# Row transpositions at the seam of image attention and output stage: which engine empties a block, in which order, and from which PSUM pool

## Chip, cores and metric

One core of a Trainium2 chip. The metric is the device time of one execution in microseconds, given as the median of several runs; the profile is one further execution on the same chip type, recorded by the hardware profiler.

## What is computed

The reference passes an image batch `x` of 4 x 56 x 56 x 128 through four layers, each added to its input after a group norm: `x = x + layer(gn(x))`. Layer 0 is a window attention with an MLP, layer 1 an edge and node layer, layer 2 a Fourier operator block with an attention over images, layer 3 a convolution along one axis with sums over rows and columns. The change lies in layer 2, between these lines and what follows them:

```python
attn_w = jax.nn.softmax(scores, axis=-1)
out = jnp.einsum('bhts,bhsd->bhtd', attn_w, vs)       # image attention, in the spectral domain here
...
projd = _fno_layer(out, wP, wPs, bPs, (H, W))
attention = _inorm(projd + xa, norm_g[1], norm_b[1])  # output stage: back transform, norms, two more
an = _inorm(attention, norm_g[2], norm_b[2])          # spectral layers, Gelu, then layer 3
```

H and W are 56, the four samples have 56 images each, and everything is float32.

## The kernel before, in words

The program is a sequence of stages. `build` (L2687) runs layers 0 and 1 sample by sample, then the spectra, the scores and the softmax of layer 2, then `attend` (L1802), then `outputs` (L2630), which does the rest of layer 2 and layer 3.

`attend` goes through 24 turns (four groups of eight columns, three products, two pairs of samples). In a turn ACT copies a piece of the spectrum into a two-bank PSUM tile (`u_px`, two buffers, L1844), DVE (L1869, reading that tile) and GpSimd (L1871) multiply it by broadcast factors, and PE sums the products with the attention weights in a one-bank tile (`u_po`, two buffers, L1874). A third kind of tile (`x_po`, two banks, one buffer) serves the mixing of images beside it. The results go to `st.y`, which is 128 partitions by (pair of samples, 32 columns, real and imaginary part, 56). The last sums of a turn of the third kind are two DVE additions that read `u_po` (L1884, or L1901 after the last turn). The PSUM pool `u_ps` (8 banks) is opened and closed inside `attend`.

`outputs` opens its own PSUM pool `o_ps`: one-bank tiles `b` (two buffers) and two-bank tiles `d` (three buffers). It describes its work as some 790 steps, each with an engine, steps that it must follow, and tiles that it takes and gives back; the list `OUTPUT_ORDER` fixes the order in which the steps are issued, and so the order on each engine. PE, ACT, DVE and GpSimd each work through their queue in that order and wait by semaphores where they need another engine's result.

The first steps belong to `attended_rows` (L2569). For each pair of samples it transposes `st.y` in four blocks of eight columns: one PE step of eight transpositions into a `d` tile (L2586), then four copies out of it (L2593), one for each half sample, into that half's tile `o_y` of 112 x 28 x 32. The copies of one block alternate: ACT, DVE, ACT, DVE. Steps 0, 5, 10 and 15 are the transpositions of the first pair, 20, 25, 30 and 35 those of the second; the four numbers after each are its copies.

`half_sample` (L2067) then works on each of eight half samples: a load of the mixed images into `o_a` (L2260, on SP's queue, 0.8 MB as rows of 56 values), a copy of one row of constants into `o_y` on ACT (`put_dc`, L2265), a transform over h on PE (L2114), its copy to SBUF on ACT (L2272), a transform over c on PE (L2131), a DVE sum with `o_a` (L2281), a transform over w on PE (L2145), the spectral products (L2167), the norms (L2198, L2225), and so on. `put_dc` is entered as following all sixteen copies of its pair of samples. Between the first and the second pair's transpositions the first three half samples advance; near the second pair's, ACT also has a root (L2302) and two Gelus with their table loads (L2336), whose result the next transform over w (L2145) reads. The large loads of `x` (L2347) are issued on SP after the second pair's transpositions.

## Time and profile before

| | |
|---|---|
| median of 3 runs | 3626.33 us |
| the runs | 3609.95, 3626.33, 3628.69 us |
| the profiled execution's own time | 3623.46 us |
| its span | 3621.7 us |
| busy in the span: PE, DVE, ACT, GpSimd | 3401.0, 2706.0, 2091.6, 1247.4 us |
| from 3254 us to the end (output stage): PE, DVE, ACT, GpSimd | 337.14, 227.82, 145.45, 222.53 us of 368 us |
| granted PE clock, before and after 3254 us | 0.98, 0.91 |

Times in the profile are microseconds from the span's start. A line of a timeline gives the start, the length, the engine, the source line, the operation, the tile written and those read, the shapes and how many instructions were merged; in brackets stands the idle time of the engine before it and what released it. A float32 matmul appears as two records (two passes), a transposition as one. Tile names lose their buffer numbers.

### The profile page before, as it was taken

To read this page: it belongs to the slowest core of one execution; us is meant where nothing else is said; L and a number is where in the kernel's file an instruction comes from. 1 tells how busy PE (TensorE), PEld (TensorE's weight loads), DVE (VectorE), ACT (ScalarE), POOL (GpSimd) and SP (SyncE) were. 2 spreads that over 40 slices of the span, in tenths; PEclk is the share of its full clock that TensorE was granted. 3 is DMA by queue.
4 is the path that set the end of the run, shared out by engine and by line. 5 is a ranking of instruction groups with operands and counts; after the bars stand their busy time and mean duration, and the time that the engine had idled before them with its cause. 6 is when DMAs were issued, how large, how long until landed. Compare 5 with 4: busy or idle time off the path is not lost.

```text
span 3621.7 us, 80884 instructions
## 1 busy us (share of the span) xinstructions
PE 3401.0 (94%) x36096; PEld 1567.0 (43%) x36096; DVE 2706.0 (75%) x2532; ACT 2091.6 (58%) x2103; POOL 1247.4 (34%) x751
## 2 busy tenths in 40 slices
PE   6999998999999898999989899999898989999998
PEld 4433344553333455333346543334466433336664
DVE  6588859758887786788859658885965768885756
ACT  4688865458887555788856468886542012215432
POOL 1000018500000660000038200001854768874766
PEclk9999999999999999999999999999998999999989
DMA  2243320024442002344400034332021047742201
GB/s 102 48 92 87 91 41 20 20 57 92 93 92 62 20 3 54 76 95 96 93 19 3 20 87 93 87 88 53 26 66 33 1 108 187 181 107 79 63 10 54
DMA packets 98496, 244.51 MB, mean 68 GB/s; under 512 B 64540, under 2 KB 69916, under 8 KB 93244
## 3 DMA queue, kind: packets, MB, share of 16 engines
q0 software_dynamic: 16128, 102.77, 14.0%
q1 hardware_dynamic: 75152, 123.61, 11.6%
q10 hardware_dynamic: 6860, 12.88, 1.3%
q8 instruction: 285, 4.67, 0.5%
q14 instruction: 71, 0.58, 0.0%
HBM read 79.46 MB, written 31.33 MB: 31 GB/s over the span
## 4 chain that ended last, share of the span: by engine, by line
PE 78%; DVE 10%; ACT 4%; issue 4%; POOL 3%; DMA 0%; DVEq 0%; POOLq 0%; SPq 0%; ACTq 0%
PE f_pm L818 17%; PE f_pm L684 15%; PE u_po L1874 8%; PE e_acc L1238 7%; PE q_acc L1732 3%; DVE e_td L1231 3%; PE f_pm L791 2%; PE e_po L1206 2%; PE f_pm L770 2%; ACT f_ring L821 1%; PE o_d L2548 1%; PE f_pm L464 1%; PE o_d L2145 1%; DVE f_acc L673 1%; PE f_pm L715 1%
## 5 line engine op out<-in xcount | busy, mean ns | idle before, releaser
L821 ACT ACTIVATE f_ring<-f_pm 128x1792 f32<-128x1792 f32 (+1 forms) x764 | 1093.9, 1482 | 228.6 <-PE f_pm L818 181.1
L673 DVE TENSOR_TENSOR f_acc<-f_acc,f_ring 128x1792 f32<-128x1792 f32 x468 | 947.7, 2025 | 191.1 <-ACT f_ring L821 160.9
L818 PE MATMUL f_pm<-f_qT,f_kT 32*128 32x448 f32 x5376 | 725.1, 571 | 15.5 <-ACT f_ring L821 5.1
L684 PE MATMUL f_pm<-f_ring,f_va 128*32 128x448 f32 (+1 forms) x6304 | 589.4, 490 | 0.0
L663 POOL DMA_DIRECT2D f_far<-f_ring x112 | 96.6, 862 | 1329.4 <-ACT f_ring L821 1087.9
L1231 DVE TENSOR_TENSOR e_td<-e_pa,e_c 128x1792 f32<-128x1792 f32 x252 | 491.1, 2018 | 14.1 <-ACT e_a L1196 14.1
L1233 POOL TENSOR_TENSOR e_tp<-e_a,e_c 128x1792 f32<-128x1792 f32 x140 | 451.5, 3263 | 101.5 <-PE e_acc L1238 60.0
L818 PEld LDWEIGHTS f_pm<-f_qT,f_kT 32*128 32x128 f32 x5376 | 260.0, 183 | 417.5 <-ACT f_ring L821 305.0
L1238 PE MATMUL e_acc<-e_td,t_shared 32*32 32x448 f32 x8064 | 325.9, 544 | 24.9 <-DVE e_td L1231 24.1
L684 PEld LDWEIGHTS f_pm<-f_ring,f_va 128*32 128x32 f32 x6304 | 163.8, 109 | 410.1 <-issue 397.8
L1869 DVE TENSOR_TENSOR u_ud<-u_px,u_d 112x1792 f32<-112x1792 f32 (+1 forms) x145 | 264.9, 1859 | 43.3 <-PE u_po L1874 35.9
L1235 ACT ACTIVATE e_tp<-e_tp 128x1792 f32<-128x1792 f32 x140 | 233.4, 1694 | 74.0 <-POOL e_tp L1233 74.0
L1871 POOL TENSOR_TENSOR u_up<-xh,u_d 112x1792 f32<-112x1792 f32 (+1 forms) x71 | 238.8, 3390 | 50.4 <-PE u_po L1874 36.3
L1238 PE MATMUL e_acc<-e_tp,t_shared 32*32 32x448 f32 x4480 | 222.8, 544 | 3.1 <-ACT e_tp L1235 2.4
L1874 PE MATMUL u_po<-u_ud,AT 112*64 112x448 f32 x1060 | 218.1, 549 | 6.4 <-issue 6.4
L1238 PEld LDWEIGHTS e_acc<-e_td,t_shared 32*32 32x32 f32 x8064 | 142.2, 103 | 138.5 <-DVE e_td L1231 79.5
L1874 PEld LDWEIGHTS u_po<-u_ud,AT 112*64 112x64 f32 x1060 | 75.6, 139 | 136.8 <-issue 122.5
L1717 POOL TENSOR_TENSOR q_u<-iS,q_g 128x1792 f32<-128x1792 f32 x32 | 102.8, 3236 | 64.9 <-PE s_px L1565 41.8
L1250 ACT COPY e_sums<-e_acc 128x1792 f32<-128x1792 f32 x28 | 46.3, 1652 | 136.4 <-PE e_acc L1238 136.4
L1238 PEld LDWEIGHTS e_acc<-e_tp,t_shared 32*32 32x32 f32 x4480 | 96.7, 103 | 52.9 <-issue 16.4
L728 DVE RECIPROCAL f_den<-f_den 128x448 f32<-128x448 f32 x28 | 82.6, 2951 | 44.1 <-ACT f_den L725 44.1
L1874 PE MATMUL u_po<-u_up,AT 112*64 112x448 f32 x476 | 105.1, 554 | 9.0 <-POOL u_up L1871 9.0
(525 smaller groups left out, 4557.0 us busy)
## 6 DMA issues: line engine op xcount, KB each, us to landing
f_far<-f_ring POOLq DMA_DIRECT2D x112, 896.0 KB, 6.3
u_d<-dd SPq DMA_DIRECT2D x44, 784.0 KB
f_far<-f_ring SPq DMA_DIRECT2D x28, 896.0 KB
xw<-in_x SPq DMA_DIRECT2D x4, 1568.0 KB
x2d<-x SPq DMA_DIRECT2D x4, 1568.0 KB
xat<-x SPq DMA_DIRECT2D x4, 1568.0 KB
x_xs<-xat ACTq DMA_DIRECT2D x32, 196.0 KB
xm<-x_ev ACTq DMA_DIRECT2D x64, 98.0 KB
```

The lines of the kernel that those rows point to most:

```text
L673: nc.vector.tensor_add(e.acc, e.acc, slots(j, c))
L684: nc.tensor.matmul(e.po[heads[h], part], va[o, c, heads[h]], p, start=(c == 0), stop=(c == 23 and part.stop == NB))
L818: nc.tensor.matmul(ss[:, i, :NB], kT[heads[h], c * P:(c + 1) * P], qT[heads[h], blk(j)], start=True, stop=True)
L821: nc.scalar.activation(ring[:, slot:slot + m, :], ss[:, :m, :NB], AF.Exp, scale=scale)
L1231: nc.vector.tensor_tensor(t, am, cm, ALU.max)
L1233: nc.gpsimd.tensor_sub(t, bc(a.rearrange("p (l n) -> p l n", l=8), 1, 4), cm)
L1235: nc.scalar.activation(tf, tf, AF.Relu)
L1238: nc.tensor.matmul(acc[quarters[q], r, :NB], k.ident[o, o], t[o, q].rearrange("p l n -> p (l n)"), start=(g == 0), stop=(g == len(EDGE_TUR ...
L1732: nc.tensor.matmul(acc[bp][i][halves[hb % 2], hb // 2, :NB], x[o], u[o, 8 * hb:8 * hb + 8, :].rearrange("p h t -> p (h t)"), start=first, ...
L1869: nc.vector.tensor_mul(u, bc(px[:, :, :NB], 2, m), dm)
L1871: nc.gpsimd.tensor_mul(u, bc(x, 2, m), dm)
L1874: nc.tensor.matmul(po[64 * b2:64 * b2 + 64, :NB], st.AT[:, 8 * i + h0 + q, 2 * bp + b2, :], u[:, b2, q, :], start=(left == 16), stop=(left ...
```

## The change

Three things, all in the two places where `st.y` is transposed, and in the PSUM pools.

1. Each block is emptied by one engine. For the first pair of samples, blocks 0 and 2 (columns 0 and 16) go to ACT and blocks 1 and 3 to DVE; for the second pair, blocks 0 and 3 go to ACT and 1 and 2 to DVE. The number of copies on each engine is the same as before (eight and eight for each pair).
2. Order. `put_dc` of a half sample follows that half's four copies alone. In the list of steps, each block's copies stand together, the third block's copies are mixed with the fourth's and with `put_dc`, and the first transform over h (step 42) stands directly after the first half's copies.
3. One PSUM pool `l2_ps`, opened in `build`, serves both stages. `u_px` and two of three `d` tiles share a tag with two buffers, `x_po` and every third `d` tile one with one buffer, `u_po` and `b` one with two.

```diff
-def attend(k, I, w, st, dd, xat, xm, softmax, beside):
+def attend(k, I, w, st, dd, xat, xm, softmax, beside, psum):
...
-        psum = es.enter_context(tc.tile_pool(name="u_ps", bufs=2, space=PSUM))
...
-            return psum.tile([P, 2, 512], F32, name="x_po", bufs=1)
+            return psum.tile([P, 2, 512], F32, tag="x", name="x_po", bufs=1)
...
-            px = psum.tile([112, 2, 512], F32, name="u_px")
+            px = psum.tile([P, 2, 512], F32, tag="px", name="u_px")[:112]
...
-            po = psum.tile([P, 512], F32, tag="acc", name="u_po")
+            po = psum.tile([P, 512], F32, tag="b", name="u_po")
...
-    @op("ACT", 0.2, rows.ops + [load_a])
+    @op("ACT", 0.2, rows.of[me] + [load_a])
     def put_dc():
...
+        dve = c0 in ((16, 8) if bp else (8, 24))
...
-            L.pt = pools.psum.tile([P, 2, 512], F32, tag="d", name="o_d", bufs=3).rearrange("p i (c t) -> p (i c) t", c=4)
+            L.pt = pools.banks().rearrange("p i (c t) -> p (i c) t", c=4)
...
-        for i, (b, half) in enumerate(units):
-            def copy_rows(i=i, b=b, half=half, c0=c0, L=L):
+        for b, half in units:
+            def copy_rows(b=b, half=half, c0=c0, L=L, dve=dve):
...
-                (nc.vector.tensor_copy if i % 2 else nc.scalar.copy)(o, L.pt[:112, :, at:at + T])
-            rows.ops.append(plan.add("DVE" if i % 2 else "ACT", 0.4, copy_rows, [p], (), [d]))
+                (nc.vector.tensor_copy if dve else nc.scalar.copy)(o, L.pt[:112, :, at:at + T])
+            rows.ops.append(plan.add("DVE" if dve else "ACT", 0.4, copy_rows, [p], (), [d]))
+            rows.of.setdefault((b, half), []).append(rows.ops[-1])
...
-0 40 119 227 306 10 3 2 1 4 5 13 12 11 14 15 6 9 7 8 18 19 16 17 41 228 120 42 307 121 43 45 44 122 124 229 47
+0 40 119 227 306 5 10 1 2 3 4 6 7 8 9 15 11 16 41 42 12 17 120 13 18 228 14 19 307 121 43 45 44 122 124 229 47
...
-239 73 149 147 74 76 240 20 150 247 25 24 23 22 21 248 77 35 29 27 30 28 37 36 39 26 38 82 31 32 33 34 78 151 83
+239 73 149 147 74 76 240 20 150 247 25 21 22 23 24 248 77 35 26 27 28 29 30 36 37 38 39 82 31 32 33 34 78
+151 83
...
-def outputs(k, w, st, ys, x2d, xm, out):
+def outputs(k, w, st, ys, x2d, xm, out, psum):
...
-        pools.psum = es.enter_context(tc.tile_pool(name="o_ps", bufs=2, space=PSUM))
-        opened = []
+        opened, taken = [], [0]
+
+        def bank():
+            return psum.tile([P, 512], F32, tag="b", name="o_b")
+
+        def banks():
+            taken[0] += 1
+            tag, bufs = ("x", 1) if taken[0] % 3 == 0 else ("px", 2)
+            return psum.tile([P, 2, 512], F32, tag=tag, name="o_d", bufs=bufs)
+        pools.bank, pools.banks = bank, banks
...
+            psum = es.enter_context(tc.tile_pool(name="l2_ps", bufs=2, space=PSUM))
-            attend(k, I, w2, st, dd, xat, xm, last_softmax, conv_weights(k, w2, l2p))
+            attend(k, I, w2, st, dd, xat, xm, last_softmax, conv_weights(k, w2, l2p), psum)
...
-        outputs(k, w2, st, ys, x2d, xm, out)
+        outputs(k, w2, st, ys, x2d, xm, out, psum)
```

More of the change, by code (lines that the diff above doesn't have):

```diff
@@ L2072, in half_sample @@
     nc = k.nc
-    wk, psum = pools.wk, pools.psum
+    wk, bank, banks = pools.wk, pools.bank, pools.banks
     T, G = HH // 2, HH // 8
@@ L2085, in tile_of @@
         return wk.tile(shape, F32, tag=tag, name="o_" + tag, bufs=plan.buffers.get(tag, 6))
-    def bank():
-        return psum.tile([P, 512], F32, tag="b", name="o_b", bufs=2)
-    def banks():
-        return psum.tile([P, 2, 512], F32, tag="d", name="o_d", bufs=3)
     def slots(x, i):
@@ L2438, in last_layer @@
     nc = k.nc
-    wk, psum = pools.wk, pools.psum
+    wk, bank, banks = pools.wk, pools.bank, pools.banks
     V = Env()
@@ L2445, in buf @@
         return n, (b, count[0])
-    def bank():
-        return psum.tile([P, 512], F32, tag="b", name="o_b", bufs=2)
-    def banks():
-        return psum.tile([P, 2, 512], F32, tag="d", name="o_d", bufs=3)
     def tile_of(shape, tag):
@@ L2574, in attended_rows @@
     rows.y, rows.ops, first = {}, [], []
+    rows.of = {}
     units = [(2 * bp + b2, half) for b2 in range(2) for half in range(2)]
```

## The prediction

> **What bounds the kernel now.** I read the busy shares first, then the chain of waits around the end of the image attention, then the timelines of PE, ACT and DVE there, and last the granted clock in windows.

> ```profile
> PE 3401.0 (94%) x36096; PEld 1567.0 (43%) x36096; DVE 2706.0 (75%) x2532; ACT 2091.6 (58%) x2103; POOL 1247.4 (34%) x751
> ...
> PE 78%; DVE 10%; ACT 4%; issue 4%; POOL 3%; DMA 0%; DVEq 0%; POOLq 0%; SPq 0%; ACTq 0%
> ```

> The kernel is bound by PE, so a gap of PE is worth its length. The change touches two places, both in the output stage that begins at 3254 us: the transpositions for samples 0 and 1, right at the seam, and those for samples 2 and 3, near 3302 us. PE's timeline at the first:

> ```profile
> 3250.92 3.18 PE L1874 MATMUL u_po<-u_ud,AT 112*64 112x448 f32 x16
> 3255.44 2.81 PE L2586 MATMUL o_d<-t_shared,y 128*112 128x128 f32 x24 [1.35 <-DVE y L1901]
> 3259.07 1.06 PE L2586 MATMUL o_d<-t_shared,y 128*112 128x128 f32 x8 [0.83 <-DVE o_y L2593]
> 3263.37 6.28 PE L2114 MATMUL o_d<-t_images,o_y 112*128 112x112 f32 x28 [3.23 <-ACT o_y L2265]
> 3269.57 1.60 PE L2131 MATMUL o_d<-o_v,t_images 32*128 32x392 f32 x16
> ```

> The bracket is the idle time before the row and its releaser. PE stands 1.35 us for DVE's last sums of the attention, 0.83 us for a free bank, 3.23 us for the row copies. Then 28 records of L2114 take 6.28 us, where 14 take 1.81 us elsewhere. The copies, two rows of ACT and two of DVE:

> ```profile
> 3256.66 0.56 ACT L2593 COPY o_y<-o_d 112x224 f32<-112x224 f32 x1 [22.40 <-PE o_d L2586]
> 3257.83 0.91 ACT L2593 COPY o_y<-o_d 112x224 f32<-112x224 f32 x2 [0.62 <-DVE o_y L2593]
> 3257.25 0.55 DVE L2593 COPY o_y<-o_d 112x224 f32<-112x224 f32 x1 [1.95 <-ACT o_y L2593]
> 3258.40 0.91 DVE L2593 COPY o_y<-o_d 112x224 f32<-112x224 f32 x2 [0.60 <-ACT o_y L2593]
> ```

> The two engines never overlap on a block; each waits 0.6 us for the other. The second place:

> ```profile
> 3305.81 1.08 PE L2586 MATMUL o_d<-t_shared,y 128*112 128x128 f32 x8 [0.81 <-ACT o_y L2593]
> 3309.23 5.17 PE L2145 MATMUL o_d<-t_images,o_t 128*128 128x64 f32 x28 [2.34 <-ACT o_y L2593]
> 3314.33 3.00 PE L2131 MATMUL o_d<-o_v,t_images 32*128 32x392 f32 x16
> ```

> Here L2145 takes 5.17 us against 3.34 us in later rows, L2131 3.00 against 1.60. The windows say why (columns: stretch, length, busy time of PE, PEld, DVE, ACT, POOL, then granted clock, DMA share, GB/s):

> ```profile
> 3255.83:3259.24 3.41, 2.58 (x25) 2.37 (x23) 1.39 (x3) 1.46 (x3) 0.00 (x0) 1.00 1.28 246
> 3259.24:3262.66 3.42, 0.90 (x8) 0.65 (x6) 1.83 (x5) 1.83 (x4) 0.00 (x0) 1.00 1.32 214
> 3307.04:3310.45 3.41, 1.22 (x11) 1.22 (x11) 0.62 (x2) 3.06 (x7) 0.13 (x2) 1.00 0.76 243
> 3365.06:3368.48 3.42, 1.96 (x10) 0.84 (x12) 3.42 (x5) 0.30 (x2) 3.42 (x2) 1.00 0.00 0
> 3460.60:3494.80 34.20, 33.88 (x158) 25.28 (x160) 14.52 (x34) 12.41 (x17) 12.27 (x9) 0.50 0.00 0
> ```

> The windows at 3259 and 3307, in which PE was busy 0.90 and 1.22 us, are each followed by 6.83 us at clock 0.50 (3262.66 to 3269.49, 3310.45 to 3317.27). Those with 1.96 or 2.58 us busy are not. The last line is a half-clock stretch that lasts 34 us although PE is hardly idle in it.

> [...] here 2.4 us of transpositions filled the window at 3255.83 and the clock stayed at 1.00, so I count them as busy. [...]

> **The change part by part, first place.** Times are on the clock of the profiled execution.

> One PSUM pool. The first transpositions read columns finished long before; what they wait for is the closing of the attention's pool, whose last reader is DVE L1901. In the built program's waits this one is gone, since their buffers are those of the attention's older tiles. They start behind the last L1874, at 3254.10 instead of 3255.44: 1.35 us. Nothing else in the attention's instruction rows or waits differs, so no cost there. The same three large buffers turn in the same order of taking, so nothing new comes to wait for a bank.

> One engine for each block. A copy costs 0.55 us alone; two in a row 0.91, three 1.28, so 0.37 us for each further one and 1.66 us for four. First copy 1.22 us after its block's first transposition (3256.66 less 3255.44). ACT: block 0 from 3255.32 to 3256.98. DVE: block 1 from about 3256.2 (its transpositions begin 0.86 us later), past L1901, which ends at 3255.3, to 3257.9. PE: fourth block, waiting for ACT's fourth copy, at 3257.1, copied from 3258.3.

> Copies in order of use. L2114 of the first unit needs one copy of each block: the third block's on ACT ends near 3257.6, the one-row copy L2265 near 3257.8, the fourth block's first on DVE at 3258.85. L2114 starts at 3258.95 instead of 3263.37: 4.42 us, of which 1.35 the pool. Behind it on ACT stand three copies and three L2265, about 2.1 us, done before 3260.2; the next one on ACT, L2272, needs L2114 and not before 3260.9. They cost nothing; without that cover up to 2 us. Added waits: each L2265 now waits for a copy on its own engine; before shows no such wait, so between 0 and 0.2 us each, I take 0.1, under the same cover.

> The clock. With gaps of 0.2 and 0.85 us no 3.41 us window falls below 2.3 us of work, so the half-clock stretch goes: two L2114 take 3.55 us and end at 3262.50. L2131 starts then instead of 3269.57: 7.07 us, of which 2.65 the clock. ACT's L2272 (0.87 us) ends at 3261.9, in time.

> What is late next: the DVE sums L2281 at 3264.2 need the first of four o_a loads (0.80 MB each). All four move at about 217 GB/s from 3255 to 3269.7, 3.7 us apiece, so the first lands near 3258.7 if they go in order. It isn't binding.

> **Second place.** The row copies here are no longer mixed. ACT: its root at 3304.07, four copies to 3305.73, so the fourth block starts at 3305.8 as before. The Gelu table load and Gelu end at 3308.02 as before. L2145 waits for that and a bank, which DVE now empties by 3306.2 instead of ACT after the Gelu. It starts at 3308.07 instead of 3309.23: 1.16 us. Idle is then 0.8 and 1.1 us; the worst window holds about 1.45 us of work, between 1.22 (halved) and 1.96 (not), most positions more. I take it that the clock stays: 1.83 us of L2145 and 1.40 us of L2131, 3.2 us. Bounds: 0 and 3.4 (half of 6.83). The last copies end at 3309.7 on ACT and 3308.7 on DVE, before L2131 needs their banks.

> Sum: 7.07 + 1.16 + 3.2 = 11.4 us. PE is busy nearly without a gap from 3311 to 3345, and the chain stays closed through POOL and DVE to the end; order and loads move along, as the large loads of x are issued after the transpositions. So all passes through. Profiled execution: 3623.46, span 3621.7 with 1.8 us around it; after, 3612.0. It is 2.9 us below the median of 3626.33; from the median, 3615.

> **Rivals.** (a) Only the second clock stretch stays: 8.2 us, 3618. For it: 1.45 lies near 1.22; against: few positions of the window are that bad. (b) The four loads share the engines and land together at 3269.8: L2281 starts 1.3 us earlier, not 7; with 4.4 us of the second place, 5.7 us, 3621. Against it: one queue, issued over 10.4 us. (c) The long half-clock stretch at 3460 doesn't come up: PE is on the chain all through it, so up to 17 us more, 3598. For it: the runs lie at 3609.95, 3626.33 and 3628.69, about one such stretch apart. (d) Slower: shifting the work by 11 us against windows that run by themselves raises another such stretch elsewhere in the output stage. Price 17 us, 3632. It ends slower once new half-clock time on PE's path exceeds twice the gain, 23 us. (e) The change does nothing: the copies' mutual waits are gone from the built program, so I give it none.

> **How the numbers follow.** Forecast 0.50 (its own range 3608 to 3622, the scatter of medians), a 0.20, b 0.10, c 0.12, d 0.08. The range 3600 to 3627 leaves out most of d and half of c with some tails. Half a per cent is 18 us, about what a measurement of this kernel can tell from no change: faster than 3608.2 is c and a tail of the forecast, 0.19; slower than 3644 0.02; within, 0.79.

> **What would show it.** Right: L2586 following L1874 without idle; L2593 in runs of four on each engine with no mutual wait; L2114 within 5 us of L1874's end at 275 ns a record; clock 1.00 through both places; L2145 about 1.2 us sooner after L2586. Wrong: L2281 released by a DMA, a clock of 0.50 at the first seam, or the gain at L2131 given back before the end on POOL or DVE.

## The result, and the profile after

| | before | after |
|---|---|---|
| median of the runs made together (8 and 8) | 3619.31 us | 3599.23 us |
| their range | 3609.95 to 3628.69 | 3593.61 to 3601.48 |
| profiled execution, its span | 3623.46, 3621.7 | 3597.24, 3595.4 |
| output stage, from the last `u_po` matmul to the end | 367.58 us | 337.70 us |
| PE busy in it, idle in it | 337.05, 30.53 us | 311.38, 26.32 us |

The ratio is 0.9943, with a 95% interval of 0.9925 to 0.9961. The forecast was 3615, range 3600 to 3627: the gain was larger than forecast, and the time fell just below the range. The page's busy line and chain of waits say as little as before, since PE is still busy for 94% of the span, and is 78% of the chain:

```profile
PE 3379.8 (94%) x36096; PEld 1550.4 (43%) x36096; DVE 2703.9 (75%) x2532; ACT 2090.7 (58%) x2103; POOL 1247.8 (35%) x751
```

The same number of PE instructions takes 21.2 us less. That is no wait removed: it is the clock, which stood at half for 195.2 us of the profiled execution before and for 151.7 us of that after. PE's timeline at the first place (the lines of the file have moved: L2586 is now L2575, L2593 is L2582, L2114 is L2107, L2131 is L2124, L2145 is L2138, L2265 is L2258):

```profile
3254.55 3.18 PE L1873 MATMUL u_po<-u_ud,AT 112*64 112x448 f32 x16
3257.66 2.83 PE L2575 MATMUL o_d<-t_shared,y 128*112 128x128 f32 x24
3260.67 1.08 PE L2575 MATMUL o_d<-t_shared,y 128*112 128x128 f32 x8 [0.18 <-ACT o_y L2582]
3262.43 3.35 PE L2107 MATMUL o_d<-t_images,o_y 112*128 112x112 f32 x28 [0.67 <-issue]
3265.71 1.60 PE L2124 MATMUL o_d<-o_v,t_images 32*128 32x392 f32 x16
```

The three waits (1.35, 0.83 and 3.23 us) have become 0, 0.18 and 0.67, and the 28 records of the transform over h take 3.35 us instead of 6.28. The copies there, two rows of ACT and two of DVE:

```profile
3258.91 2.18 ACT L2582 COPY o_y<-o_d 112x224 f32<-112x224 f32 x5 [21.03 <-PE o_d L2575]
3260.88 0.24 ACT L2258 COPY o_y<-dc 1x28 f32<-1x28 f32 x1
...
3259.66 1.71 DVE L2582 COPY o_y<-o_d 112x224 f32<-112x224 f32 x4 [0.73 <-PE o_d L2575]
3261.80 1.71 DVE L2582 COPY o_y<-o_d 112x224 f32<-112x224 f32 x4 [0.42 <-PE o_d L2575]
```

ACT and DVE now work at the same time, each four copies in 1.7 us, and wait for PE alone. The second place on PE:

```profile
3301.83 1.08 PE L2575 MATMUL o_d<-t_shared,y 128*112 128x128 f32 x8 [0.71 <-ACT o_y L2582]
3302.75 0.33 PE L2138 MATMUL o_d<-t_images,o_t 128*128 128x64 f32 x2
3304.09 3.12 PE L2138 MATMUL o_d<-t_images,o_t 128*128 128x64 f32 x26 [1.01 <-ACT o_t L2329]
3307.13 1.60 PE L2124 MATMUL o_d<-o_v,t_images 32*128 32x392 f32 x16
...
3331.15 3.34 PE L2138 MATMUL o_d<-t_images,o_t 128*128 128x64 f32 x28 [0.66 <-DVE o_a L2390]
```

L2138 starts before the Gelu has ended, with its first two records, and its main part starts 2.26 us after the fourth block began instead of 3.42. The last line is a wait that before didn't have: PE, now ahead, stands 0.66 us for DVE. Then the clock, for the stage as a whole and for the work that had the long half-clock stretch (columns: stretch, length, busy time of PE, PEld, DVE, ACT, POOL, clock, DMA share, GB/s):

```profile
3453.00:3487.00 34.00, 33.45 (x292) 23.59 (x296) 23.09 (x52) 18.99 (x26) 20.92 (x14) 1.00 0.01 1
...
3257.70:3595.40 337.70, 311.38 (x2234) 203.69 (x2232) 226.19 (x398) 144.27 (x207) 222.48 (x136) 0.99 0.20 58
```

In 34 us of this work before issued about 158 PE instructions at clock 0.50, and after issues 292 at 1.00. Comparing when the same PE instruction starts, counted from the beginning of the stage: after is ahead by 7.50 us at the first L2124, by 12.23 behind the second place, by 11.5 once the 0.66 us wait has come, and by that much up to 206 us of the stage. There before begins its half-clock stretch of 34.1 us, and when it ends after is ahead by 26.75. Two short stretches of before, near 302 and 316 us of the stage, make it 29.9. In the stages ahead of the seam, after's profiled execution was 3.6 us slower, which leaves the 26.3 us by which the spans differ.

### The profile page after: what moved, and what is told of

Same layout as the page of the kernel before. It is cut to its first block, busy times and chain, and to the rows that moved or that the text cites. A ratio compares the mean times of both kernels' runs of the same rounds, so it can differ in the third digit from the quotient of the medians.

```text
span 3595.4 us, 80880 instructions
## 1 busy us (share of the span) xinstructions
PE 3379.8 (94%) x36096; PEld 1550.4 (43%) x36096; DVE 2703.9 (75%) x2532; ACT 2090.7 (58%) x2103; POOL 1247.8 (35%) x751
## 4 chain that ended last, share of the span: by engine, by line
PE 78%; DVE 10%; ACT 4%; issue 4%; POOL 2%; DMA 0%; DVEq 0%; POOLq 0%; SPq 0%; ACTq 0%
PE f_pm L818 17%; PE f_pm L684 15%; PE u_po L1873 8%; PE e_acc L1238 7%; PE q_acc L1732 3%; DVE e_td L1231 3%; PE f_pm L791 2%; PE e_po L1206 2%; PE f_pm L770 2%; ACT f_ring L821 1%; PE f_pm L464 1%; PE o_d L2138 1%; DVE f_acc L673 1%; PE o_d L2535 1%; PE f_pm L715 1%
## 5 line engine op out<-in xcount | busy, mean ns | idle before, releaser
L818 PE MATMUL f_pm<-f_qT,f_kT 32*128 32x448 f32 x5376 | 725.1, 571 | 15.5 <-ACT f_ring L821 5.1
```

The source lines that it names most:

```text
L818: nc.tensor.matmul(ss[:, i, :NB], kT[heads[h], c * P:(c + 1) * P], qT[heads[h], blk(j)], start=True, stop=True)
```

## Experiments

Theory 1: what the change does at its two places is worth some 12 us, as forecast; the rest is the long half-clock stretch, which before would have in only a part of its executions and after in none. In each trace the half-clock stretches begin on a grid of 3.41 us (3413.3 ns, read below), and where the stage lies against this grid, whose steps are called windows here, decides which half-clock stretches come later. Rivals: that one part of the change, for instance the shared pool, carries the gain alone; that the stretch comes by chance and was absent from after's runs by luck; that a delay costs just its length.

**The kernel before once more.** No edit.

> The kernel before, unchanged, profiled once more. The eight runs of it fall into two groups, four at 3610 to 3614 us and four at 3625 to 3629 us, 13.7 us apart. Theory 1, a clock lottery: the half-clock stretch of 34 us near 3460 us, which costs 15.2 us on PE, is present in the upper group alone. Then an execution below 3616 us shows no such stretch and a mean clock near 0.977, one above 3622 us shows it and 0.973. Theory 2: the stretch belongs to the order of work, every execution has it, and the two groups come from the stages before 3254 us; then the stretch is there whatever the time.

Measured: 3615.39 us (3608.69 to 3627.93, 14 runs), ratio 0.9997 [0.9982, 1.0013]. Its profiled execution took 3616.84, between the two bounds of the expectation and nearer to the lower group, with a stage of 356.1 us, 11.5 shorter than that of the profile of before. The same work as in the long stretch, in this execution's windows:

```profile
3465.50:3499.70 34.20, 32.15 (x282) 23.16 (x282) 22.65 (x50) 18.94 (x25) 22.26 (x15) 1.00 0.01 2
```

The identical program ran here at clock 1.00, so the stretch isn't in every execution. Over all 149 runs of the kernel before in this study, 94 lie below 3619 us with a median of 3612.6, and 55 above with a median of 3626.2; the mean clock, which is on record for 141 of them, is 0.974 to 0.978 in the first group and mostly 0.971 to 0.973 in the second. The median of all is 3614.9. Two of the three runs that the forecast started from, and its profile, were of the upper group. That the long stretch makes the upper group is read from one trace with it (3623.46 us) and one without; no other execution of this kernel has a trace.

**The parts.** Four kernels: the shared pool alone; the first pair's copies and order alone; the second pair's alone; and all copies and orders without the shared pool.

Against the kernel after, the first lines undo the copies (for both pairs in the first kernel, for one in the next two), and the last two undo the pool (in all but the first kernel):

```diff
-    @op("ACT", 0.2, rows.of[me] + [load_a])
+    @op("ACT", 0.2, rows.ops + [load_a])
...
-        for b, half in units:
-            def copy_rows(b=b, half=half, c0=c0, L=L, dve=dve):
+        for i, (b, half) in enumerate(units):
+            on_dve = bool(i % 2)
+            def copy_rows(b=b, half=half, c0=c0, L=L, dve=on_dve):
...
-            return psum.tile([P, 2, 512], F32, tag=tag, name="o_d", bufs=bufs)
+            return own.tile([P, 2, 512], F32, tag="d", name="o_d", bufs=3)
```

The list of steps is that of before wherever copies are undone. With the second pair alone, each `put_dc` still follows all sixteen copies of its pair.

> The shared PSUM pool alone, copies and order as before. Both theories: PE starts the transpositions behind the last matmul of the attention, 1.3 us sooner. The copies still take turns, so the gap behind the transpositions stays near 3.2 us and the clock is halved: L2131's counterpart starts 1.3 us sooner against the stage's start. Theory 1: the times fall into the same two groups, each 1.3 us lower, ratio 0.9965 to 1.003. Theory 2: as the stretch is tied to the order of work, which is unchanged, it shows in the profile in any case.

> One engine for each block and the order of use for the first pair of samples alone, the second pair and the pools as before. By the steps of the prediction: 3.1 us from copies and order, about 2.65 us from the clock at the first place, 5.7 to 6.2 us at the first transform over c counted from the stage's start; the second place is unchanged at its start, its clock stretch may stay. Theory 1: the long stretch comes or not by chance. Theory 2: it is set off by the work at 3460 us and stays.

> One engine for each block and the order for the second pair alone, the first pair and the pools as before. By the steps of the prediction: 0 us at the first place, 1.2 us at the second transposed pair's next transform over w, and up to 3.2 us more if the clock stays at 1.00 there; 1.2 to 4.5 us in all. Theory 1 and 2 on the long stretch as for the run of the first pair alone.

> The change without its shared PSUM pool: copies, order and waits as in the changed kernel, but each stage with a pool of its own. By the steps of the prediction the transpositions start 1.3 us later and everything behind moves by that, 3600.5 us. Theory 1b: the long half-clock stretch is no chance but comes where the small matmuls behind 195 us of the stage stand at a certain place of the 3.41 us window (0.09 of a window in the profile before, 0.70 in the profile after). A shift of 1.3 us is 0.38 of a window and brings them to 0.08, so the stretch comes in a third or more of the executions, then near 3615 us, the rest near 3600. Theory 1a: pure chance with the rate of before, 16 of 50, whatever the shift. Theory 3: the changed kernel is free of it for another reason, and all executions stay near 3600 us.

| | median us (range, runs) | ratio to before [95%] | less the lower group of before beside it | runs above 3619 |
|---|---|---|---|---|
| pool alone | 3611.61 (3606.55 to 3617.26, 22) | 0.9984 [0.9974, 0.9995] | -1.0 | 0 |
| first pair alone | 3605.55 (3601.10 to 3613.81, 12) | 0.9967 [0.9953, 0.9981] | -7.0 | 0 |
| second pair alone | 3606.47 (3603.64 to 3626.28, 15) | 0.9981 [0.9965, 0.9997] | -6.1 | 3 |
| without the pool | 3603.95 (3600.25 to 3606.16, 6) | 0.9951 [0.9933, 0.9969] | -9.2 | 0 |
| all (the kernel after) | 3599.23 (3593.61 to 3601.48, 8) | 0.9943 [0.9925, 0.9961] | -13.1 | 0 |

The fourth column takes out the share of the upper group in the runs of before: their median below 3619 us was 3612.3 beside the kernel after, 3612.6 beside the first three kernels, 3613.2 beside the fourth.

PE's timelines, of the pool alone and then of the first pair alone:

```profile
3254.59 2.83 PE L2575 MATMUL o_d<-t_shared,y 128*112 128x128 f32 x24
3258.25 1.06 PE L2575 MATMUL o_d<-t_shared,y 128*112 128x128 f32 x8 [0.83 <-DVE o_y L2583]
3262.54 5.01 PE L2107 MATMUL o_d<-t_images,o_y 112*128 112x112 f32 x28 [3.23 <-ACT o_y L2258]
```

```profile
3255.02 2.80 PE L2575 MATMUL o_d<-t_shared,y 128*112 128x128 f32 x24 [1.34 <-DVE y L1900]
3258.01 1.09 PE L2575 MATMUL o_d<-t_shared,y 128*112 128x128 f32 x8 [0.19 <-ACT o_y L2583]
3259.77 3.35 PE L2107 MATMUL o_d<-t_images,o_y 112*128 112x112 f32 x28 [0.67 <-issue]
```

Each part removes just the waits that the forecast gave it. The pool takes away the 1.35 us; it leaves 0.83, 3.23 and a half-clock stretch (of one window, 3.4 us). The first pair's copies take away 0.64 and 2.56 us and the half clock. So no single part carries the gain. The totals don't seem to add: the three parts alone are worth 1.0, 7.0 and 6.1 us, the two sets of copies together 9.2 and not 13.1, and the pool on top of them 3.9 and not 1.0. Each of these figures is uncertain by 2 us or more, by the scatter of its runs, so the times alone don't show this; the traces do. In these kernels the upper group is gone wherever the first place was touched, also with the pool alone, whose share at the first place is 2.7 us: the runs of the pool alone, of the first pair alone, of the kernel without the pool and of the kernel after lie within 6 to 13 us each (48 runs in all), which leaves no room for a second group 13.6 us higher. So its absence from the runs of after is not luck. One expectation did not come true: without the pool the long stretch should have stayed in a third of the runs and came in none of six, which at a third would still happen once in eleven times. The second place shows why the parts needn't add. Without the pool, its waits are those of after, and yet:

```profile
3308.50:3315.30 6.80, 6.80 (x33) 4.11 (x34) 1.60 (x2) 3.84 (x3) 0.00 (x0) 0.50 1.02 437
3302.00:3308.50 6.50, 4.79 (x42) 4.40 (x41) 3.76 (x11) 6.09 (x13) 0.22 (x2) 1.00 0.33 85
```

Idle is 1.71 us (6.50 less 4.79), as in after (0.71 and 1.01), and a half-clock stretch of 6.8 us follows; in after none does.

**Delays.** If position decides, pure delay at the seam must sometimes cost much more than its length, and a delay longer by one window must cost as if the window weren't there. Filler matmuls, whose result goes nowhere, were put behind the first pair's fourth block (the numbers of fillers in one sketch):

```diff
+            if bp == 0 and c0 == 24:
+                fill = pools.bank()
+                for c in range(6):            # 2, 6, 10 or 11
+                    nc.tensor.matmul(fill[:, :384], k.ident, w.W.rearrange("p t c -> p (t c)"), start=True, stop=True)
+                # 2 and 256, 6 and 256, 11 and 128: one more of so many columns
```

The same in the kernel before, with nine fillers in its 3.23 us wait, closes the gap without the change.

> The kernel before with nine matmuls of 384 columns more behind the fourth block of transpositions of the first pair, 2.9 us in the 3.2 us in which PE waited for the row copies. Nothing else is changed. If idle windows halve the clock at the seam, as the prediction has it, the 6.83 us at 0.50 are gone, the first two transforms over h take 3.55 us instead of 6.28, and the first transform over c starts 2.65 us sooner, at 12.8 instead of 15.5 us from the stage's start. If transpositions or fillers don't count for the clock, it starts at 15.5 us still. The second place is unchanged.

Measured: 3610.86 us (3608.32 to 3616.96, 18 runs), ratio 0.9978 [0.9967, 0.9988]. The half-clock stretch at the seam is gone although no wait was shortened:

```profile
3263.52 5.97 PE L2590 MATMUL o_b<-t_w_W,t_shared 128*128 128x384 f32 x18
3269.33 3.28 PE L2114 MATMUL o_d<-t_images,o_y 112*128 112x112 f32 x28
```

L2114 takes 3.28 us instead of 6.28, and the clock from 3266 to 3273 us is 1.00. So the low activity ahead of it (0.90 us of PE in the window from 3259.24 us of the profile of before) did set off that stretch. The fillers took 5.8 us in a gap of 3.2, twice the author's estimate of 2.9, so L2131 started only 0.6 us sooner. No run lies above 3619.

> The changed kernel with six matmuls of 384 columns more behind the fourth block of transpositions of the first pair. Their result is read by nothing. They take 1.9 us, of which 0.7 us fills idle time, so the rest of the stage moves by 1.25 us with the clock kept: 3600.5 us by the sum. Theory 1b: the small matmuls come to 0.07 of a window, the long stretch comes in a third or more of the executions, 3615 us for those. Theory 1a: as often as at any other shift. Theory 3: none.

> The same with ten matmuls, 3.2 us: the rest of the stage moves by 2.5 us, 3601.8 us by the sum. Theory 1b: the small matmuls come to 0.44 of a window, where the second profile of the kernel before (0.39) had no long stretch, so no execution has it. Theory 1a: as often as at any other shift, a third. Theory 3: none.

> The kernel after, with 6 filler matmuls of 384 columns and one of 256 behind the last transpositions of the first pair (their result goes nowhere): a delay of about 3.4 us of the whole output stage, which is one window of the clock (3.41 us). Theory 1 (the position of the stage against the windows decides which half-clock stretches come): the stage lies against the windows as in the kernel after, so it takes its stretches (the last one alone, about 10 us) and the time is that of after plus 3.4, about 3602.6 us, which is about 8 us faster than the kernel with six fillers (3610.7) although its delay is longer. Rival theory 2 (a delay costs what it takes and half-clock stretches come by chance or with the length of the filler): 3610 us or more, with stretches near 180 and 299 us of the stage as with six fillers.

> The kernel after, with 11 filler matmuls of 384 columns and one of 128 at the same place: a delay of about 6.4 us, that of the kernel with six fillers (3.0) and one window of the clock. Theory 1: the half-clock stretches of the kernel with six fillers come back (10 us each near 50, 180 and 299 us of the stage), and the time is about 3614 us, 10 us above the kernel with ten fillers (3604.5), for a delay only 0.9 us longer. Rival theory 2: the time of ten fillers plus 0.9 us, about 3605.5 us, without stretches near 180 and 299 us.

> The kernel after, with 2 filler matmuls of 384 columns and one of 256 at the same place: a delay of about 0.85 us, a quarter of a window. Theory 1 does not say which stretches this position brings, only that they may be others than in the kernel after: a time between 3600 us (none new) and 3614 us (those of six fillers and more). Rival theory 2: 3600.1 us and the stretches of the kernel after.

The fillers in the kernel after also took twice as long as the author's estimates in the first two expectations (3.87 us for six, against 1.9), so the delays below are those read from the traces, at the first L2124. With six fillers, none of the three theories of its expectation came true: the runs lie neither near 3600.5 us nor in part near 3615 with the long stretch, and the trace has other stretches. The three expectations after those of six and ten fillers rest on the position of the whole stage.

| delay at L2124, us | less whole windows | median us (range, runs) | ratio to before [95%] | less the lower group of before beside it | added to after, less the delay |
|---|---|---|---|---|---|
| 0 (after) | 0 | 3599.23 | 0.9943 [0.9925, 0.9961] | -13.1 | 0 |
| 0.83 | 0.83 | 3605.17 (3598.91 to 3613.10, 15) | 0.9970 [0.9957, 0.9982] | -6.5 | 5.8 |
| 2.97 | 2.97 | 3610.69 (3605.38 to 3623.06, 22) | 0.9977 [0.9967, 0.9987] | -2.5 | 7.6 |
| 3.40 | -0.01 | 3601.38 (3598.26 to 3605.78, 8) | 0.9965 [0.9952, 0.9977] | -10.3 | -0.6 |
| 5.56 | 2.15 | 3604.47 (3600.67 to 3606.32, 6) | 0.9952 [0.9934, 0.9970] | -8.7 | -1.2 |
| 6.42 | 3.01 | 3612.66 (3605.45 to 3618.16, 14) | 0.9993 [0.9982, 1.0004] | 1.0 | 7.7 |

The rows of 2.97 and 5.56 us were run side by side (lower group 3613.2), and so were those of 0.83, 3.40 and 6.42 (lower group 3611.7). Within each set a longer delay is faster: 5.56 us beats 2.97 by 6.2 us, 3.40 beats 0.83 by 3.8; and 6.42 is 11.3 slower than 3.40 for 3.0 us of delay. Two delays that differ by one window cost the same beyond their length, as far as runs that scatter by 2 or 3 us can tell: 7.6 and 7.7, 0 and -0.6. The rival that a delay costs its length is out. One of the 22 runs with six fillers lies far above the others, at 3623.06 us; its trace wasn't taken. In the traces, six fillers and then eleven and a part have their stretches at the same work, 3.5 us apart in the stage (179.2 and 182.7, 298.7 and 302.2). Windows of the kernel with six fillers (the first is the window just ahead of the stretch near 180 us), and those of the kernel with ten at the work near 180:

```profile
3435.03:3438.44 3.41, 3.41 (x32) 3.18 (x28) 2.42 (x6) 3.39 (x4) 3.41 (x3) 1.00 0.02 5
3438.44:3448.64 10.20, 10.20 (x35) 5.78 (x33) 7.19 (x8) 1.67 (x5) 10.08 (x5) 0.50 0.40 79
3557.90:3568.10 10.20, 8.88 (x20) 4.58 (x19) 6.88 (x10) 0.30 (x1) 9.71 (x7) 0.50 0.00 0
```

```profile
3440.00:3450.00 10.00, 9.63 (x66) 5.50 (x66) 9.58 (x12) 1.70 (x4) 9.92 (x7) 1.00 0.06 10
```

The position can be read in every trace, since all half-clock stretches of one execution begin on one grid of 3413.3 ns, within some 10 ns. The mark is the `o_wr` matmul row that starts at 146.7 us of the stage in the profile of before (3400.83); the position is its distance from the grid's last line. The last stretch, some 10 us at the end of the stage, is in every trace and is left out:

| kernel | position of the mark, us of 3.41 | half clock behind it, us | from the mark to the end, us |
|---|---|---|---|
| after | 0.34 | none | 202.5 |
| eleven fillers, six fillers, pool alone | 1.40, 1.45, 1.50 | 17.0, 20.4, 20.4 (near 180 and 300) | 207.5, 209.3, 209.2 |
| before with fillers near 206 us (below) | 1.59 | 20.5 (near 183 and 295) | 211.8 |
| before | 1.65 | 44.3 (near 206, 302 and 316) | 220.8 |
| second pair alone, without the pool, first pair alone, before with fillers at the seam | 2.00, 2.00, 2.07, 2.11 | 3.4 in each (near 285) | 203.8, 203.7, 203.7, 203.8 |
| ten fillers, six and a part | 2.47, 2.53 | 3.4 in each (near 280) | 203.9, 203.9 |
| before once more | 2.70 | 6.8 | 204.7 |
| two fillers and a part | 2.86 | 10.2 | 205.7 |

Kernels at nearly the same position have much the same stretches, whatever their edits: the three up to 1.50 have two, near 180 and 300 us, and the six from 2.00 to 2.53 one of a single window. The exception is at 1.59 and 1.65, where two traces of a program that is the same up to 206 us differ. Work from the mark on is the same in all fourteen, up to the added fillers, and it takes 202.5 to 205.7 us outside positions 1.40 to 1.65, and 207.5 to 220.8 within.

That a delay shows in medians at all needs one thing more. The executions begin anywhere on the grid (0.06 to 2.77 us behind one of its lines), and yet eleven of the fourteen enter the output stage at 1.44 to 1.81 us. The first pair alone and the delays of 0.83 and 3.40 us enter it at 0.13, 0.22 and 0.39, and the traces of these two delays are of the slowest runs of their kernels (3613.10 and 3605.78 us). So the mark of the delay of one window stands at 2.53 in its trace and not near the 0.34 of after: that it costs nothing beyond its length is shown by its times, not by its trace. How the work ahead of the seam brings most executions to one position was not tried.

**What sets off the long stretch.** It begins in the profile of before at 3460.6 us, in a 1.20 us wait of PE:

```profile
3460.92 0.98 PE L2198 MATMUL o_b<-o_t,c_ones 112*32 112x224 f32 x8 [1.20 <-ACT o_t L2187]
```

Two fillers were put into that wait:

```diff
+            if name == "q" and me == (2, 0):
+                for c in (384, 256):
+                    nc.tensor.matmul(ps[:, :c], k.ident, w.W.rearrange("p t c -> p (t c)")[:, :c], start=True, stop=True)
```

> The kernel before, with two filler matmuls of 384 and 256 columns in the 1.2 us for which TensorE waits near 206 us of the output stage, where the long half-clock stretch of the profiled execution began. Theory 1b (the low activity at that place sets off the long stretch in the runs that have it): no run above 3622 us any more, where about a third of the runs of the kernel before lie; the other runs stay near 3612 us or rise by less than 1 us, so that the median falls by 2 to 4 us to about 3612 us. Rival 1c (the long stretch is set off elsewhere, or by what the windows before hold): about a third of the runs stay above 3622 us and the median stays at 3615 us or above.

Measured: 3612.71 us (3608.09 to 3618.20, 14 runs), ratio 0.9992 [0.9979, 1.0005]. No run lies above 3619; of the 38 runs of before made beside them ten do. If the share had stayed at ten in 38, fourteen without one would come about once in 70 times. Everything up to that wait is the program of before, so this speaks for the long stretch being set off there, by the low activity; with fourteen runs it is not beyond chance. The median didn't fall as expected: it is equal to that of before beside it (3612.65, itself low, with its lower group at 3611.7). That is 1 us above the lower group, which is within the scatter. The trace shows that another stretch can come first:

```profile
3436.30:3453.40 17.10, 17.10 (x62) 10.21 (x61) 9.53 (x13) 2.70 (x7) 12.57 (x7) 0.50 0.47 92
3467.00:3487.00 20.00, 19.45 (x165) 14.54 (x165) 14.16 (x34) 9.98 (x14) 11.47 (x8) 1.00 0.01 2
```

The first line is a stretch of five windows near 183 us of the stage, ahead of the fillers, with PE busy throughout; the second, from the fillers on, is at clock 1.00.

**What the windows held.** A gap of PE isn't the whole cause: the line of six fillers above shows a window in which PE was busy for all of 3.41 us, followed by half clock. The traces allow a count that fits better. For each window of the grid, add up the columns of its matmul records, each weighted by the size of its weights as a share of 128 x 128, the largest in any record: a record `128*128 128x448` counts 448, a record `128*32 128x392` counts 98. No window holds more than 4118. Over all fourteen traces, with limits that were chosen from the counts themselves:

| weighted columns in a window | at full clock: the next one at half, at full | at half clock: the next one at half, at full |
|---|---|---|
| under 1300 | 319, 12 | 289, 16 |
| 1300 to 1600 | 38, 60 | 34, 73 |
| 1600 and more | 0, 13575 | 0, 254 |

Busy time separates them less well: of the windows at full clock with 1.4 to 3.0 us of it, 73 were followed by half clock and 1259 were not, and of those with PE busy throughout, five were, each with 1428 to 1554 columns. The count also fits with a stretch that lasts: the ten windows of the long stretch hold 612 to 1441 columns, those of the same work in after, at full clock, 1649 to 2871. The window ahead of the long stretch holds 1495 in before, which is on the edge, and that before the same wait 1672 in before once more. By this count the position would act by where the grid cuts the gaps and the matmuls with few columns. The count was made on traces already at hand; no run was built to test it.

## Why the forecast was off

| step of the sum | forecast us | measured us | read from |
|---|---|---|---|
| pool, first transposition | 1.35 | 1.3 | no idle ahead of L2575 |
| copies in order, by one engine | 3.07 | 3.3 | L2107 4.70 us after the stage begins, before 9.27 |
| clock at the first place | 2.65 | 2.9 | 28 records in 3.35, before 6.28 |
| bank of the next transform over w | 1.16 | 1.16 and about 0.4 | 2.26 after 3.42; two records early, 0.10 less wait |
| clock at the second place | 3.2 | 3.1 | 5.17 to 3.45, 3.00 to 1.60 |
| sum of both places | 11.4 | 12.2 | position behind the second place |
| a wait for DVE, new | 0 | -0.7 | L2138 waiting for L2390 |
| long half-clock stretch | 0 (rival c, 0.12) | 15.2 | stage 206 to 241 us |
| two later stretches | 0 | 3.1 | near 302 and 316 us |
| stages ahead of the seam | 0 | -3.6 | stage starts at 3257.7, before 3254.1 |

The mechanism at both places was right, term by term, but for the reason given for the clock at the second (below), and what would show it did show: L2107 within 5 us, copies in runs without mutual wait, clock 1.00 at both places, the shared pool's wait gone. The order of releases was right too: each `put_dc` took 0.10 us between its neighbours (it starts at 3260.88 us, the next copy at 3260.98), as the forecast estimated, under cover. Rival (b) is out: the DVE sum L2274 waited for PE and not for a load.

The step that failed is "So all passes through". It took the rest of the stage as fixed, with its long half-clock stretch moved along by 11 us. The stretch did not move along: it was there with the mark at 1.65 us of the grid (before), and in the profiled execution after, with the mark at 0.34, it is absent, which is worth 15.2 us there. That was rival (c), named with its price (3598) and given 0.12. What the forecast quoted for it, runs "about one such stretch apart", was a sign of two things: that the stretch is not in every execution, and that the base of 3626.33 was drawn mostly from the group that has it. From the median of all 149 runs, 3614.9, the gain is 15.7 us; from the lower group, 3612.6, it is 13.4, 2.0 above the sum of 11.4 (13.1 with the runs made beside the kernel after). Of the 15.8 us by which the forecast missed, 11.4 are the base (3626.33 less 3614.9). The other 4.4 would be the removal of the upper group (2.3, from 3614.9 to 3612.6) and of short stretches (about 2, no more than the scatter). The table above shows more, 15.2 and 3.1, because the profiled execution of before stood in the upper group.

The term for the second place was right in this kernel but for a weaker reason than given. The forecast held that a window with at least 1.45 us of work would keep the clock. Of eight kernels that have the change's second pair, five have a half-clock stretch of 3.4 to 10.2 us there (second pair alone, without the pool, and three with fillers), three none. The windows just ahead of those five hold 1.68 to 2.45 us of PE time, above that bound. The forecast had taken it from single windows; in the same profile others with 1.9 to 2.3 us, near 203, 299 and 312 us of the stage, are followed by half clock. That the clock stayed at 1.00 here was thus in part luck of position: the lowest window of after at this place holds 1651 weighted columns, just above the mixed range of 1300 to 1600. Rival (a) was thus not a question of the gap's length alone, and 0.20 was too little for it. Rival (d) is the same mechanism with the other sign. It is real: a delay of 3.0 us cost 10.6 (7.6 and its length). It did not come for this change, but nothing in the profile of before excluded it.

The forecast let the clock's windows run by themselves in rival (d) and not in its sum. The traces show them so: in each of the fourteen executions one grid of 3413.3 ns carries all half-clock stretches, and the execution begins anywhere from 0.06 to 2.77 us behind one of its lines. A busy PE alone did not bring the full clock back: PE was busy for 17.10 of 17.10 us (before with fillers near 206 us) and for 33.88 of 34.20 (before) at clock 0.50, in windows of fewer than 1600 weighted columns.

Left open: why windows of 1300 to 1600 weighted columns go either way, and whether this count is what the clock goes by; why two engines that read one block in turn waited for each other; how far the shares of the two groups depend on what runs ahead of the seam, where 130 to 154 us of half clock lie in each trace; and whether a position with fewer stretches than that of after exists. None of these was tried. None of the kernels beats the kernel after.

## What to carry to other kernels

In these traces a gap of PE that left a window of 3.41 us at full clock with under 1.4 us of work was followed by half clock in 279 of 279 cases, for at least one window, so such a gap cost more than its length. Closing it took the second cost away even where the work was thrown away: with nine fillers at the seam the 28 records behind them took 3.28 us instead of 6.28. Windows with PE busy throughout were followed by half clock too in five cases, each with 1428 to 1554 weighted columns of matmuls with small weights or few columns. Moving the output stage by a few microseconds changed which later gaps and small matmuls were followed by half clock: a delay of 2.97 us cost 7.6 us beyond its length, one of 3.40 us -0.6. So a sum of waits is good to about 10 us here even where each term is right to 0.5. Before a small effect is forecast from a median of a few runs, look whether these fall in groups, which group the profile is from, and what clock each has.
